# A four-layer cross-attention network with expert layers: expert outputs of layers 1 and 3 written to token rows in DRAM by accumulating scatters, weights carried beside the rows, layer 3 dispatched by ranks

## The chip, the core and the metric

The kernel runs on one core of a Trainium2 chip. The metric is device time in microseconds for one execution. Before the change it was 4479.0 as the median of three runs (4478.08 to 4484.96). Names of engines are those of the profile: PE multiplies matrices (PEld loads its weights), DVE, ACT and POOL work on vectors, SP issues DMAs. POOL issues every indirect DMA, that is, a DMA whose rows are addressed by a list of indices.

## What is computed

Four layers work on x, 2048 tokens of 256 float32. Each layer adds a cross-attention over a context of 1601 rows (16, 16, 8 and 16 heads) and then a feed-forward part with experts. A layer norm stands ahead of each. The feed-forward parts of layers 1, 2 and 3 are, cut to what matters here:

```python
# layer 1: top 2 of 8 experts, all pairs kept
topk_values, topk_indices = jax.lax.top_k(x @ router_w, 2)
topk_weights = softmax(topk_values)
h1 = gelu(einsum('bth,efh->btef', x, w1) + b1)
expert_outputs = einsum('btef,ehf->bteh', h1, w2) + b2
out = sum over the two of expert_outputs[chosen] * topk_weights
# layer 2: 8 experts
y = einsum('bsi,eoi->bseo', x, We) + be
out = einsum('bseo,bse->bso', y, gate_sparse)          # two nonzero gates a token
# layer 3: a shared MLP, and top 2 of 16 experts with room for 320 pairs each
pos = (cumsum(oh_e, axis=0) * oh_e).sum(axis=1) - 1    # place of a pair at its expert
within = pos < 320
expert_outputs = vmap(mlp)(expert_inputs, w_gate, w_up, w_down)   # silu(x wg) * (x wu) wd, F = 352
out = x + mlp(x, shared) + sum over the two of expert_outputs[chosen] * vals * within
```

Layer 0 has a shared MLP and 16 experts, all of them computed for all tokens.

## The kernel before

x stays in SBUF as four blocks of 512 tokens (NB = 4), each of four tiles of 128 tokens (NT = 4). PE's order within attention is written out by hand (`tc.manual_schedule`), and so is the interleaving of the next attention's start (`lead`) with the end of a feed-forward part. The rest is ordered by a scheduler at build time. [...]

Layer norm: `norm_rows` (L399) makes the normed rows xn of a block on POOL: rs, pow, then four subtract-and-multiply (L406), one for each tile. PE transposes them (L416), and the router's logits follow (L621). For the last block of a layer nothing else is left for PE to do meanwhile.

Layer 1. `ffn1` sorts the 4096 pairs of token and expert by expert into 40 tiles of 128 places (TL1 = 40, some places empty). PE counts pairs by matmuls of the one-hot matrix (L913 to L916); `locate` (DVE) finds which row of counts a place falls into; `tokens` gathers four rows `rk` of ranks (L1028, POOL) and makes token numbers out of them; `pairs_T` gathers 128 normed rows `xg` (L1047, POOL), PE transposes them (L1055) and DVE copies (L1057). `hidden` is L1067 and the GELU L1075, `down` is L1089; DVE copies the result (L1093), and SP stores it in `ys_dram` (L1094). The expert's weights w1 and w2, 1 MB each, are fetched by indirect DMAs (L966, POOL) two tiles ahead into two buffers each; where the buffer already holds the same expert the indices are out of bounds and nothing moves. In sixteen of the 40 tiles `bias` (L1113) also adds one token tile's combination of expert biases: a transpose (L767), a copy (L769), a matmul (L771) and a sum into x (L772). When all tiles are done, `combine` (L1140) gathers, for each token tile, its two rows of `ys_dram` (L1144, POOL) and adds them with their weights (L1150, DVE). The next attention's `lead` is interleaved with it.

Layer 2. `ffn2` begins with the biases of all sixteen token tiles (`add_biases`, L774, by the same lines L767 to L772) and then computes all experts (L1174).

Layer 3. `ffn3` counts pairs on PE (L1221), finds each pair's place on DVE and scatters token numbers into a `table` in DRAM by 32 indirect DMAs (L1264), each of which waits for the one before, since they write to the same tensor. The shared MLP runs meanwhile (L1305 and L1323). The table is read back as `slots` (L1280). For each of 16 experts, three indirect DMAs gather normed rows (L1338), PE transposes (L1348), `mlp_hidden` runs (L1305, ACT L1309, DVE L1312), then down (L1357), DVE's copy (L1364) and SP's store (L1365). At the end 32 indirect DMAs gather the two results of each token (L1372), DVE adds them (L1378) and SP stores x as the output.

Of the kernel before, what the change touches and what calls it, by code (L numbers as in the profile page):

```python
# [66 lines left out]
def block_stack(ctx: ExitStack, tc: tile.TileContext, I: dict, out: bass.AP):  # L67
# [44 lines left out]
    iota_p = slot_id[:, 0:1]  # L112
    iota_t = const.tile([P, TL1], F32, name="iota_t")
# [285 lines left out]
    def norm_rows(b, mv):  # L399

        rs = small.tile([P, NT], F32, tag="rs", name="rs")
        nc.gpsimd.tensor_scalar(rs, mv[:, :, 1], LN_EPS, None, ALU.add)  # L402
        nc.gpsimd.tensor_tensor(rs, rs, neg_half, ALU.pow)
        xn = act.tile([P, NT, D], F32, tag="xn", bufs=1, name="xn")
        for t in range(NT):
            nc.gpsimd.tensor_scalar(  # L406
                xn[:, t, :], x[b][:, t, :], mv[:, t, 0:1], rs[:, t : t + 1], ALU.subtract, ALU.mult
            )
        return xn
# [21 lines left out]
    def attention(L, W, kT, V, after):  # L431
# [68 lines left out]
        def rows(b):  # L500
            xn[b] = norm_rows(b, mvs.pop(b))
# [158 lines left out]
    def two_hot(eng, cw, i8f, w, E):  # L660

        o = onehots(i8f, 2, E)
        for k in range(2):
            eng.tensor_tensor(o[:, k], o[:, k], w[:, :, k : k + 1].to_broadcast([P, NT, E]), ALU.mult)
# [13 lines left out]
    def weights_tile(b, E):  # L678
        return small.tile([P, NT, E], F32, tag=f"cw{b}", bufs=1, name=f"cw{b}")
# [85 lines left out]
    def add_bias(b, t, cw, be, E):  # L765
        pt = ps_misc()
        nc.tensor.transpose(pt[0:E, 0:P], cw, ident)  # L767
        cT = tmp([P], "cT")
        nc.vector.tensor_copy(cT[0:E, :], pt[0:E, 0:P])  # L769
        po = ps_misc()  # L770
        nc.tensor.matmul(po[:, 0:D], cT[0:E, :], be, start=True, stop=True)  # L771
        nc.vector.tensor_tensor(x[b][:, t, :], po[:, 0:D], x[b][:, t, :], ALU.add)  # L772

    def add_biases(b, cw, be, E):  # L774

        for t in range(NT):
            add_bias(b, t, cw[:, t, :], be, E)
# [19 lines left out]
    def work(name):  # L797
        return act.tile([P, 2, BT], F32, tag="work", bufs=6, name=name)

# [86 lines left out]
    def ffn1(chosen, xn_dram, fill, lead):  # L886
# [6 lines left out]
        b2 = wp.tile([E, D], F32, tag="be", name="b2")  # L893
        nc.sync.dma_start(b2, I["b2"])
# [11 lines left out]
        oh, w = chosen  # L906

        both = act.tile([P, NTT, E], F32, tag="mp", name="both")
        nc.vector.tensor_tensor(both, oh[0], oh[1], ALU.add)
        bothf = both.rearrange("p t e -> p (t e)")  # L910
        NE = NTT * E
        prow, ptot, pin = ps_one(), ps_one(), ps_one()
# [3 lines left out]
        nc.tensor.matmul(pin[:, 0:NE], upper, bothf, start=True, stop=True)  # L916
# [74 lines left out]
        tile_of, row = cut(TL), cut(TL)  # L991
        row_u, tok_u = cut(TL, U32), cut(TL, U32)

        def locate(t0, n):
# [20 lines left out]
            nc.vector.tensor_tensor(rank[:, at], rank[:, at], before, ALU.subtract)  # L1015
            nc.vector.tensor_scalar(tile_of[:, at], tile_of[:, at], NTT - 1.0, None, ALU.min)
# [6 lines left out]
        def tokens(t0, n):  # L1023
# [18 lines left out]
            nc.vector.tensor_scalar(tok[:, 0:n], tok[:, 0:n], T - 1.0, None, ALU.min)  # L1042
            nc.vector.tensor_copy(tok_u[:, at], tok[:, 0:n])

        def pairs_T(t):
            xg = act.tile([P, D], F32, tag="xnT", bufs=5, name="xg")
# [11 lines left out]
            return xT  # L1058
# [24 lines left out]
        ys_dram = dram.tile([TL * P, D], F32, name="ys1_dram")  # L1083

        def down(t, h):
# [7 lines left out]
            nc.vector.tensor_copy(ys, pd[:, 0:D])  # L1093
            nc.sync.dma_start(ys_dram[t * P : (t + 1) * P, :], ys)  # L1094


        place = act.tile([P, NTT, E], F32, tag="mp", name="place")
        nc.vector.tensor_tensor(
            place, pin[:, 0:NE].rearrange("p (t e) -> p t e", e=E), cum, ALU.add
        )  # L1100
        nc.vector.tensor_tensor(place, place, tot, ALU.subtract)
        nc.vector.tensor_tensor(place, place, bc(st, NTT), ALU.add)
        slots = []
        for k in range(2):
            pk = act.tile([P, NTT, E], F32, tag="mp", name="pk")
            nc.vector.tensor_tensor(pk, place, oh[k], ALU.mult)
            sk = cut(NTT)
            nc.vector.tensor_reduce(sk.unsqueeze(2), pk, AX.X, ALU.add)
            sk_u = cut(NTT, U32)
            nc.vector.tensor_copy(sk_u, sk)  # L1110
            slots.append(sk_u)

        def bias(b, t):  # L1113
            at = slice(b * NT + t, b * NT + t + 1)
            cw = tmp([E], "cw_t")
            nc.vector.tensor_scalar(cw, oh[0][:, b * NT + t, :], w[0][:, at], None, ALU.mult)
            nc.vector.scalar_tensor_tensor(cw, oh[1][:, b * NT + t, :], w[1][:, at], cw, ALU.mult, ALU.add)
            add_bias(b, t, cw, b2, E)
# [4 lines left out]
        for t in range(TL + 1):  # L1123
# [5 lines left out]
            if t < TL:  # L1129
                hs[t] = hidden(t, xTs.pop(t))  # L1130
                if t + 2 < TL:
                    fetch(w1s[t % 2], "w1", t + 2)
            if t > 0:
                down(t - 1, hs.pop(t - 1))
                if t + 1 < TL:
                    fetch(w2s[(t - 1) % 2], "w2", t + 1)
            if 8 <= t < 8 + NTT:
                bias(*divmod(t - 8, NT))

        def combine(b, t):  # L1140
            tt = b * NT + t
            y = act.tile([P, 2, D], F32, tag="xnT", bufs=5, name="y")
            for k in range(2):
                nc.gpsimd.indirect_dma_start(  # L1144
                    out=y[:, k, :],
                    out_offset=None,
                    in_=ys_dram,
                    in_offset=bass.IndirectOffsetOnAxis(ap=slots[k][:, tt : tt + 1], axis=0),
                )
                nc.vector.scalar_tensor_tensor(  # L1150
                    x[b][:, t, :], y[:, k, :], w[k][:, tt : tt + 1], x[b][:, t, :], ALU.mult, ALU.add
                )

        with tc.manual_schedule(engines={mybir.EngineType.PE}):
            for tt in range(NTT):
                combine(*divmod(tt, NT))
                if tt >= NT - 1:
                    lead((tt - NT + 1) / (NTT - NT))

    def ffn2(xnT, lead):  # L1160
        E = 8
        be = wp.tile([E, D], F32, tag="be", name="be")
        nc.sync.dma_start(be, I["be"])
# [27 lines left out]
        for b in range(NB):  # L1191
            add_biases(b, cws[b], be, E)
# [9 lines left out]
    SC = [(0, P), (P, 2 * P), (2 * P, CAP)]  # L1202

    def ffn3(xnT, chosen, xn_dram):
        NTT = NB * NT
        TW = E3 * len(SC)

        table = dram.tile([P * TW, 1], I32, name="table")
        zero = const.tile([P, TW], I32, name="zero")
        nc.vector.memset(zero, 0)  # L1210
        nc.sync.dma_start(table.rearrange("(p c) o -> p (c o)", p=P), zero)
        ids = const.tile([P, NTT], I32, name="ids")
        nc.gpsimd.iota(ids, pattern=[[P, NTT]], base=0, channel_multiplier=1)

        oh, idx, w = chosen

        both = act.tile([P, NTT, E3], F32, tag="mp", name="both")
        nc.vector.tensor_tensor(both, oh[0], oh[1], ALU.add)
        bothf = both.rearrange("p t e -> p (t e)")
        pin, ptot = ps_one(), ps_one()  # L1220
        nc.tensor.matmul(pin[:, 0 : NTT * E3], upper, bothf, start=True, stop=True)  # L1221
        nc.tensor.matmul(ptot[:, 0 : NTT * E3], ones, bothf, start=True, stop=True)
# [358 lines left out]
```

## Time and profile before

The profiled execution took 4487.74 us, of which 4486.0 are the span of its instructions; the mean granted clock of PE was 0.959.

| what | us |
|---|---|
| median of three runs | 4479.0 |
| profiled execution, span | 4487.74, 4486.0 |
| busy: PE, DVE, ACT, POOL | 4258.6, 2414.3, 1959.6, 653.1 |
| layer 1, the 40 tiles | 2093.6 to 2416.7 |
| layer 2, biases | 3159.3 to 3188.5 |
| layer 3, table scatters L1264 | 4150.2 to 4231 |
| layer 3, the 16 experts | 4237.9 to 4434 |
| layer 3, gathers, sums and store | 4434 to 4486 |

A row of the profile's timeline gives start, duration, engine, line, operation and operands; in brackets stands how long the engine was idle ahead of it and what released it. A row of windows gives a stretch, its length, each engine's busy time with the number of its instructions in parentheses (PE, PEld, DVE, ACT, POOL), the granted clock of PE, the share of time the DMA engines were busy, and GB/s. The slices give the span in 40 equal parts and the busy share in tenths.

### The profile page before, as it was taken

What the parts mean: (1) busy time and instruction counts of PE and PEld (TensorE: products, weight loads), DVE (VectorE), ACT (ScalarE), POOL (GpSimd) and SP (SyncE); (2) the same over time, 40 slices, a digit from 0 to 9 for tenths busy, and PEclk for the clock granted to TensorE, in tenths of its full rate; (3) what the DMA queues carried; (4) which work ended last, traced back from release to release, by engine and by line L of the source; (5) the groups of instructions that cost most, each with busy time, mean ns of one, the idle gap of its engine ahead of it and who ended that gap; (6) DMA issues with size and microseconds to landing.
All of it is one profiled execution on the core that took longest, in us unless ns stands there. A gap on an engine that the chain in (4) does not pass through costs nothing. (4 is left out here: it accounts for less than half of the span.)

```text
span 4486.0 us, 62975 instructions
## 1 busy us (share of the span) xinstructions
PE 4258.6 (95%) x25100; PEld 1965.4 (44%) x25100; DVE 2414.3 (54%) x4911; ACT 1959.6 (44%) x3690; POOL 653.1 (15%) x833
## 2 busy tenths in 40 slices
PE   8999999999999999998996999999999999998695
PEld 4333333366543333336885433334443333333463
DVE  5776776324677776753222544451486777673122
ACT  1666655511156655662221234343016766665010
POOL 2000100100000010004445100012000001001323
PEclk8999999999999999999998799999899999999897
DMA  2000000000000000002453000000000000000144
GB/s 75 3 3 4 3 3 6 3 23 1 3 3 6 4 8 3 11 6 70 163 167 89 10 5 3 5 6 3 3 16 3 4 3 8 11 1 10 32 148 116
DMA packets 64429, 117.31 MB, mean 26 GB/s; under 512 B 20110, under 2 KB 41478, under 8 KB 59528
## 3 DMA queue, kind: packets, MB, share of 16 engines
q1 hardware_dynamic: 43272, 58.12, 4.3%
q0 software_dynamic: 20864, 55.18, 4.1%
q8 instruction: 198, 3.24, 0.3%
q14 instruction: 95, 0.78, 0.1%
HBM read 138.37 MB, written 16.88 MB: 35 GB/s over the span
## 5 line engine op out<-in xcount | busy, mean ns | idle before, releaser
L284 DVE TENSOR_REDUCE mx<-ps_m 128x1 f32<-128x512 f32 x2688 | 1699.9, 685 | 672.2 <-PE ps_m L277 437.5
L325 PE MATMUL ps_s<-q,kT 32*128 32x512 f32 (+2 forms) x5824 | 1721.0, 623 | 0.7 <-DVE mx L284 0.6
L277 PE MATMUL ps_m<-kT,q 32*128 32x512 f32 x5376 | 1604.8, 644 | 29.9 <-DMA q<-qc 18.5
L335 ACT ACTIVATE e<-ps_s 128x512 f32<-128x512 f32 (+1 forms) x2080 | 1110.7, 599 | 890.5 <-PE ps_s L325 694.4
L343 PE MATMUL ps_acc<-e,V 128*32 128x512 f32 (+2 forms) x5824 | 928.5, 609 | 6.2 <-ACT a L524 5.7
L325 PEld LDWEIGHTS ps_s<-q,kT 32*128 32x128 f32 (+2 forms) x5824 | 576.4, 180 | 671.7 <-DVE mx L284 397.0
L277 PEld LDWEIGHTS ps_m<-kT,q 32*128 32x128 f32 x5376 | 580.4, 188 | 504.4 <-issue 383.1
L333 ACT ACTIVATE e<-ps_s,mcol 128x512 f32<-128x512 f32 (+1 forms) x832 | 514.8, 686 | 224.3 <-PE ps_s L325 143.8
L343 PEld LDWEIGHTS ps_acc<-e,V 128*32 128x32 f32 (+2 forms) x5824 | 160.6, 112 | 640.6 <-issue 508.4
L266 POOL MEMSET mp<- 128x512 f32 x64 | 33.2, 525 | 1846.7 <-PE ps_m L315 1836.2
L1075 ACT ACTIVATE h<-ps_h,w 128x128 f32<-128x128 f32 x320 | 91.1, 372 | 217.7 <-issue 138.2
L854 DVE SCALAR_TENSOR_TENSOR x<-ps_m,cw,x 128x256 f32<-128x256 f32 x256 | 111.1, 479 | 102.1 <-PE ps_m L846 99.1
L402 POOL TENSOR_SCALAR rs<-mv 128x4 f32<-128x4 f32 x32 | 7.6, 239 | 1050.5 <-DVE mv L394 1050.5
L406 POOL TENSOR_SCALAR xn<-x,mv,rs 128x256 f32<-128x256 f32 x128 | 156.0, 1231 | 3.5
L1067 PE MATMUL ps_h<-xT,w 128*128 128x128 f32 x1280 | 153.2, 279 | 0.4 <-issue 0.4
L817 ACT ACTIVATE h<-ps_h 128x512 f32<-128x512 f32 x80 | 47.7, 597 | 242.3 <-PE ps_h L816 242.3
L1067 PEld LDWEIGHTS ps_h<-xT,w 128*128 128x128 f32 x1280 | 149.6, 195 | 0.8 <-issue 0.5
L301 DVE TENSOR_REDUCE mx<-ps_m 128x4 f32<-128x260 f32 x224 | 80.4, 423 | 126.0 <-PE ps_m L293 126.0
L1089 PE MATMUL ps_m<-w,h 128*128 128x256 f32 x640 | 144.6, 379 | 0.0
L1089 PEld LDWEIGHTS ps_m<-w,h 128*128 128x128 f32 x640 | 118.6, 190 | 14.5
L1312 DVE TENSOR_TENSOR h<-ps_h,sg 128x320 f32<-128x320 f32 (+3 forms) x60 | 31.8, 530 | 168.1 <-PE ps_h L1305 121.6
L816 PE MATMUL ps_h<-xnT,up 128*128 128x512 f32 x256 | 117.9, 604 | 0.0
(286 smaller groups left out, 3179.6 us busy)
## 6 DMA issues: line engine op xcount, KB each, us to landing
q<-qc SPq DMA_DIRECT2D x192, 32.0 KB
gu<-in_w_gate SPq DMA_DIRECT2D x16, 352.0 KB
gu<-in_w_up SPq DMA_DIRECT2D x16, 352.0 KB
ys_dram<-ys SPq DMA_DIRECT2D x40, 128.0 KB
xn_dram<-xn SPq DMA_DIRECT2D x8, 512.0 KB
dn<-in_w_down SPq DMA_DIRECT2D x16, 256.0 KB
ys<-ys_sb SPq DMA_DIRECT2D x32, 128.0 KB
x<-in_x SPq DMA_DIRECT2D x4, 512.0 KB
```

The costliest lines, as they stand in the source:

```text
L277: nc.tensor.matmul(pm, q1[at : at + 32, t * P : (t + 1) * P], kT[at : at + 32, g, KB[kb] : KB[kb + 1]], start=True, stop=True,)
L284: nc.vector.tensor_reduce(mx[:, t, j, kb : kb + 1], pm, AX.X, ALU.max)
L325: nc.tensor.matmul(sp, kT[j * S : (j + 1) * S, g, c * P : c * P + cw], q2[j * S : (j + 1) * S, :], start=True, stop=True,)
L333: nc.scalar.activation(e[0:cw], sp, AF.Exp, bias=mcol[0:cw, c : c + 1])
L335: nc.scalar.activation(e[0:cw], sp, AF.Exp)
L343: nc.tensor.matmul(acc[j * S : (j + 1) * S, :], V[0:cw, c, h * (d + 1) : h * (d + 1) + S], es[j // 2][0:cw, j % 2, :], start=(c == 0), sto ...
L406: nc.gpsimd.tensor_scalar(xn[:, t, :], x[b][:, t, :], mv[:, t, 0:1], rs[:, t : t + 1], ALU.subtract, ALU.mult)
L816: nc.tensor.matmul(pu, u(c), xnT[b][:, c, :], start=(c == 0), stop=(c == 1))
L854: nc.vector.scalar_tensor_tensor(x[b][:, t, :], pd[:, i * D : (i + 1) * D], cws[b][:, t, e0 + e + i : e0 + e + i + 1], x[b][:, t, :], ALU. ...
L1067: nc.tensor.matmul(pu[:, (f - f0) * P : (f - f0 + 1) * P], w1[:, c * F1 + f * P : c * F1 + (f + 1) * P], xT[:, c, :], start=(c == 0), stop ...
L1075: nc.scalar.activation(h[:, f, :], pu[:, (f - f0) * P : (f - f0 + 1) * P], AF.Gelu, bias=w1[:, 2 * F1 + f : 2 * F1 + f + 1],)
L1089: nc.tensor.matmul(pd[:, 0:D], h[:, f, :], w2[:, f * D : (f + 1) * D], start=(f == 0), stop=(f == 7))
```

## The change

Rows in DRAM get wider: behind the 256 normed values of a token stand its weights for all experts (8 in layer 1, 16 in layer 3), so that whoever gathers a row has the weight too. 128 zero rows behind the tokens are spare: empty places point there. A second tensor, `acc_dram`, holds x; experts' results, already multiplied with the weight, are added to it by indirect DMAs with `compute_op=ALU.add`, 40 in layer 1 and 48 in layer 3, each waiting for the one before. After layer 1, x is read back from it; after layer 3 it is copied to the output, DRAM to DRAM. The gathers and sums at the end of both layers, `ys_dram` and the place of each pair are gone.

Layer 3 finds its tokens as layer 1 does, by gathering ranks (40 gathers), and gathers rows for two experts at a time, five tiles of 128 for 2 x 320 places. The tile in the middle belongs half to one and half to the other. Its counting now stands behind the first block of the shared MLP.

The biases of layers 1 and 2 are added in routing, one block at a time: one transpose, an ACT copy, four matmuls and four sums. `norm_rows` takes the engine for the rows: DVE for the last block after each attention, and for the first block at the start of each.

```diff
-    def norm_rows(b, mv):
+    def norm_rows(b, mv, eng):
...
-            nc.gpsimd.tensor_scalar(
+            eng.tensor_scalar(
...
+    def add_biases(b, cw, be):
         pt = ps_misc()
+        nc.tensor.transpose(pt[:, 0:P], cw.rearrange("p t e -> p (t e)"), ident)
+        cT = small.tile([P, P], F32, tag="cT", bufs=1, name="cT")
+        nc.scalar.copy(cT, pt[:, 0:P])
+        pos = [ps_misc() for t in range(NT)]
         for t in range(NT):
-            add_bias(b, t, cw[:, t, :], be, E)
+            at = slice(t * 32, t * 32 + 8)
+            nc.tensor.matmul(pos[t][:, 0:D], cT[at, :], be[at, :], start=True, stop=True)
+        for t in range(NT):
+            nc.vector.tensor_tensor(x[b][:, t, :], pos[t][:, 0:D], x[b][:, t, :], ALU.add)
...
+    def spare(tok, gone, tok_u):
...
+        nc.vector.tensor_scalar(tok, tok, T - 1.0, None, ALU.min)
+        nc.vector.tensor_scalar(other, tok, -1.0, spare_row, ALU.mult, ALU.add)
+        nc.vector.tensor_tensor(other, other, gone, ALU.mult)
+        nc.vector.tensor_tensor(tok, tok, other, ALU.add)
+        nc.vector.tensor_copy(tok_u, tok)
...
         def pairs_T(t):
-            xg = act.tile([P, D], F32, tag="xnT", bufs=5, name="xg")
+            xg = act.tile([P, D + E], F32, tag="xnT", bufs=5, name="xg")
...
-            return xT
+            w8 = tmp([E], "w8")
+            nc.vector.tensor_tensor(w8, xg[:, D : D + E], oht[:, t, :], ALU.mult)
+            weight = small.tile([P, 1], F32, tag="weight", bufs=4, name="weight")
+            nc.vector.tensor_reduce(weight, w8, AX.X, ALU.add)
+            return xT, weight
...
-            nc.vector.tensor_copy(ys, pd[:, 0:D])
-            nc.sync.dma_start(ys_dram[t * P : (t + 1) * P, :], ys)
+            nc.vector.tensor_scalar(ys, pd[:, 0:D], weight, None, ALU.mult)
+            nc.gpsimd.indirect_dma_start(
+                out=acc_dram,
+                out_offset=bass.IndirectOffsetOnAxis(ap=tok_u[:, t : t + 1], axis=0),
+                in_=ys,
+                in_offset=None,
+                compute_op=ALU.add,
+            )
...
-            if 8 <= t < 8 + NTT:
-                bias(*divmod(t - 8, NT))
...
+        for b in range(NB):
+            nc.sync.dma_start(
+                x[b], acc_dram[b * BT : (b + 1) * BT, :].rearrange("(t p) d -> p t d", p=P)
+            )
         with tc.manual_schedule(engines={mybir.EngineType.PE}):
-            for tt in range(NTT):
-                combine(*divmod(tt, NT))
-                if tt >= NT - 1:
-                    lead((tt - NT + 1) / (NTT - NT))
+            lead(1.0)
...
-        for b in range(NB):
-            add_biases(b, cws[b], be, E)
```

Layer 3, the new functions in short, and the order in which they run:

```python
def tokens(k):
    at = slice(5 * k, 5 * k + 5)
    rk = act.tile([P, 5, P], F32, tag="o_tok", bufs=2, name="rk")
    for c in range(5):
        nc.gpsimd.indirect_dma_start(out=rk[:, c, :], in_=ranks_dram, ...)
    nc.vector.tensor_tensor(rk, rk, rank[:, at].unsqueeze(2).to_broadcast([P, 5, P]), ALU.is_le)
    ...
def pairs(k):
    ...
    for c in range(5):
        nc.gpsimd.indirect_dma_start(out=xg[c], in_=xn_dram, ...)
    ws = small.tile([P, 6], F32, tag="ws", name="ws")
    for to, c, src, two in (...):
        nc.vector.tensor_copy(ws[0 : src.stop - src.start, to : to + 1], xg[c][src, e : e + 1])
    return xg, ws
def down(k, two, hs, dn, ws):
    ...
    for i, (n, tok) in enumerate(parts):
        pd = ps_one()
        ys = act.tile([P, D], F32, tag="mp", name="ys")
        ...
        nc.vector.tensor_scalar(ys[0:n, :], pd[0:n, 0:D], w, None, ALU.mult)
        nc.gpsimd.indirect_dma_start(out=acc_dram, ..., in_=ys[0:n, :], compute_op=ALU.add)
...
for b in range(NB):
    if b == 1:
        cum = counts()
        locate(cum)
        tokens(0)
        tokens(1)
    hs = mlp_hidden(gu, [xnT[b][:, c, :] for c in range(2)], BT)
    ...
    nc.sync.dma_start(acc_dram[b * BT : (b + 1) * BT, :].rearrange("(t p) d -> p t d", p=P), x[b])
xg, ws = pairs(0)
for k in range(E // 2):
    xT = pairs_T(xg)
    ws_now = ws
    if k + 2 < E // 2:
        tokens(k + 2)
    if k + 1 < E // 2:
        xg, ws = pairs(k + 1)
    for two in range(2):
        gu, dn = load_mlp("w", 2 * k + two)
        hs = mlp_hidden(gu, [xT[c][:, two * CAP : (two + 1) * CAP] for c in range(2)], CAP)
        down(k, two, hs, dn, ws_now)
for b in range(NB):
    nc.sync.dma_start(out[b * BT : (b + 1) * BT, :], acc_dram[b * BT : (b + 1) * BT, :])
```

## The prediction

> **What bounds the kernel now.** I read the slices first, then busy time by stage, then single stretches.
>
> ```profile
> span 4486.0 us, 62975 instructions
> PE 4258.6 (95%) x25100; PEld 1965.4 (44%) x25100; DVE 2414.3 (54%) x4911; ACT 1959.6 (44%) x3690; POOL 653.1 (15%) x833
> PE   8999999999999999998996999999999999998695
> POOL 2000100100000010004445100012000001001323
> ...
> 2416.70:2438.70 22.00, 0.06 (x2) 0.04 (x1) 7.58 (x21) 0.00 (x0) 13.20 (x16) 0.57 0.34 102
> 2438.70:2497.80 59.10, 43.75 (x107) 25.18 (x108) 36.54 (x71) 1.86 (x3) 35.87 (x33) 0.53 0.18 54
> 3158.00:3189.00 31.00, 24.18 (x56) 9.88 (x55) 9.85 (x32) 0.52 (x2) 0.00 (x0) 0.60 0.00 1
> 4186.00:4237.00 51.00, 19.72 (x67) 11.94 (x65) 4.84 (x7) 1.79 (x3) 18.41 (x19) 0.72 0.09 25
> 4237.00:4434.00 197.00, 194.21 (x768) 126.23 (x768) 43.56 (x96) 34.46 (x80) 43.13 (x46) 0.98 0.45 130
> 4434.00:4486.00 52.00, 0.00 (x0) 0.00 (x0) 15.74 (x33) 0.00 (x0) 30.91 (x32) 0.53 0.41 123
> ```
>
> PE is 95% busy, so only what PE does or waits for counts. The dips are at the combine of layer 1 (2417 to 2498), the biases of layer 2 (3158 to 3189, at a granted clock of 0.60) and layer 3: waiting for the slot table until 4237, and a tail of 52 us after PE's last matmul. In layers 1 and 3 POOL, which issues every indirect DMA, is busiest.
>
> ```profile
> 4194.99 0.97 POOL L1264 DMA_INDIRECT table<-ids,at_u  x1 [1.46 <-DMA table<-ids,at_u]
> 4197.39 0.97 POOL L1264 DMA_INDIRECT table<-ids,at_u  x1 [1.44 <-DMA table<-ids,at_u]
> ...
> 4237.91 0.69 PE L1348 MATMUL ps_m<-ident,xg 128*128 128x128 f32 x2 [32.18 <-DMA xg<-xn_dram,slots]
> 4241.28 9.06 PE L1305 MATMUL ps_h<-xT,gu 128*128 128x320 f32 x24 [0.41 <-issue]
> ...
> 4255.51 6.76 PE L1305 MATMUL ps_h<-xT,gu 128*128 128x320 f32 x24
> 4438.56 0.95 POOL L1372 DMA_INDIRECT y<-ys,row_u  x1 [0.30 <-issue]
> ```
>
> Two prices: indirect DMAs that wait for each other start 2.4 us apart; those that don't, 1.27 (0.95 + 0.30). After a long idle stretch the first hidden layer takes 9.06 instead of 6.76, so a stall costs about 2 us besides its own length.
>
> **Layer norm rows on DVE.**
>
> ```profile
> 2047.11 0.69 PE L416 MATMUL ps_m<-ident,xn 128*128 128x128 f32 x2 [4.75 <-POOL xn L406]
> 2048.32 0.69 PE L416 MATMUL ps_m<-ident,xn 128*128 128x128 f32 x2 [0.52 <-POOL xn L406]
> ```
>
> For a layer's last block PE waits 4.75 + 3 x 0.52 for POOL's four rows of 1.21. A 128x256 copy on DVE takes 0.42, so four rows come 3.1 sooner; rs and pow stay on POOL. DVE has nothing else there. I take -3 per layer, four times: **-12** (0 to -14). The first block's rows matter only after layer 1, and are in that tail.
>
> **Biases.** In layer 1 sixteen tiles of the expert loop take 8.79 instead of 7.25 (transpose 0.27, wait 0.59, matmul 0.69): 24.6 leave. In layer 2, 3159.3 to 3188.5 holds nothing but sixteen transposes and biases: 29.2 leave. Added: per block one transpose 0.27, an ACT copy (about 0.4), four matmuls of 0.43: 2.5 each for three blocks inside attention, 7.5. The last block has no cover. In layer 1 its weights are made while DVE finishes routing anyway (PE already idles 2.76 before L913): 4.5. In layer 2 PE used to start the next layer's K/V projections at once, and now stands queued behind the bias; logits to cw took 3124.5 to 3130.6 with a projection's copies of some 1.6 between, so 4.5 + 2.7 = 7.2. Layer 1: -24.6 + 12 = **-12.6**; layer 2: -29.2 + 14.7 = **-14.5** (each within 6).
>
> **Layer 1 loop.** Without biases it is 323.1 - 24.6 = 298.5. POOL's four tiles held 16 indirect DMAs (4 ranks, 4 rows, 8 weight fetches) and now hold 20, with four accumulating scatters: 20 x 1.27 = 25.4 of 29.0. That fits as a sum, but the queue is in order: a scatter waits for the evacuation of its tile, and behind it stand the next fetch of w1, three rank gathers and the rows; DVE's weight products wait for those gathers and stand ahead of the evacuations. Following one period through both queues with the rows' durations gives 30.1 to 30.5 instead of 29.0: +12 over ten. At seven expert changes w1 is issued late, where 1 MB needs about 3.4 (the first four took 13.5): I take 1 each, 7 in all, less 1 for what was already late before: **+18**. Bounds: 0 (all covered) and +53 (rival d).
>
> **End of layer 1.** The 40 stores of ys, 32 gathers and 32 DVE sums go. After PE's last matmul come evacuation, scatter, a reload of x, statistics and rows. Evacuation to landing about 6, reload about 4 (a quarter of those 13.5), statistics, pow and rows on DVE about 5: the query projection at +15.6 instead of +26.7 (2416.7 to 2443.4), -11. In the stretch after, PE idles 59.1 - 43.75 = 15.4, much of it because the maxima share DVE with L1150; I take 12 of it. **-23** (-10 to -28).
>
> **Layer 3, dispatch.** Gone: 32 chained table scatters and the read of slots. Added: five count matmuls after the shared MLP's first block (about 4147), 16 sums (3.1 by L1226) and a locate, then 40 rank gathers that don't wait for each other: 4159 + 40 x 1.27 + 2 = 4212. Every one of them stands ahead of the first rows in POOL's queue: five gathers and 2.7 to land, first hidden layer at 4222 instead of 4241.3: **-19** (-8 to -24). The shared MLP is over at about 4197, so some 25 of idle PE stay.
>
> **Layer 3, loop.** Sixteen experts of 11.93 = 191. Rows are gathered five per pair of experts instead of six, the store of ys becomes 48 accumulating scatters, each waiting for the one before. Let L be their spacing. No row of this trace has an accumulate. Lower bound: 2.4, the table's scatters, with 4 bytes a row. Nearest for 1 KB rows: a gather is used by DVE 2.7 after its start (4437.29 to 4440.02); a scatter adds a read of the target. Upper bound: two such trips and the issue, 2 x 2.7 + 0.95 = 6.4. With weights filling DMA to 0.45 I take L = 4.0, nearer the single trip. POOL per pair: 6 scatters, of which one overlaps the row gathers, 5L + 6.4 = 26.4 against PE's 23.87: +2.5, over 8 pairs +20. Or, seen from DVE: the copy of the pair's last weight waits for row gather c4, which is queued behind a scatter, and h stands behind it: a scatter's trip less the 1.1 that PE is ahead, 2.9 in six pairs, 17. These are one delay, not two; with lost clock in six places, 1.5 each: **+28** (+8 at L = 2.4; +116 at L = 6.4, where POOL needs 38.4, 14.5 over PE's).
>
> [...]
>
> **Layer 3, tail.** Gone: last store, 32 gathers of y (40 us), 32 sums, the store of out. Added: the last scatters, about 10 after PE's last matmul at L = 4, then four copies of 512 KB from DRAM to DRAM; 130 GB/s at a share of 0.45 makes some 290, 2 MB in 7 plus 2 to land. 20 instead of 52: **-32** (-25 to -36).
>
> **Sum**: -12 - 12.6 - 14.5 + 18 - 23 - 19 + 28 - 32 = -67. The profiled span 4486.0 becomes 4419; its execution took 4487.74, 8.7 above the median 4479.0 of the three runs, so I expect **4412** as median.
>
> **Rivals.**
> (b) The scatter chain decides. At L = 6, POOL needs 36.4 per pair, 12.5 over PE's 23.87: +100 instead of +28, tail +6: -67 + 78 = +11, 4490; at 6.4 4507. From L = 5.7 on the change loses. For it: every table scatter waited, some 3.8 apart instead of 2.4 under load; the target is read too. Against: POOL's wait in the typical row is only 1.46. 0.18.
> (c) All is covered: L at most 2.5, the layer 1 queue as fast as PE. +8 and 0 instead of +28 and +18: -105, 4374. For it: POOL is 15% busy over the span, table scatters 2.4. Against: in layer 1 it is 45%, and order, not sum, decides. 0.14.
> (d) Layer 1's fetches come late: seven changes at 6 + 1.6 (clock; L1067 took 5.37 instead of 3.74 after a 1.64 stall) make +53 instead of +7: -21, 4458. For it: each scatter sits between two fetches in one queue. Against: two buffers. 0.13.
> My forecast gets 0.50, with its own range 4385 to 4440; 0.05 is left for a mixture near no change. Slices from (c) to (b) give 4360 to 4488. I take 0.2% (9 us) as what a measurement can tell. Faster: forecast, (c) and most of (d): 0.75; slower: 0.18; same: 0.07.
>
> **What would show it.** PE's wait before the first xg transpose of layer 3 near 20; spacing of L1416's scatters near 4, and pairs near 27; nothing but four copies after a tail of 20; the layer 1 loop near 317, with POOL fetches just before use; layer 2's biases as one 7 us stop after the logits. Wrong if a scatter takes 6 or more, or if rank gathers are still running at 4230.

## The result, and the profile after

The changed kernel takes 4519.5 us (median of four runs, 4517.94 to 4520.16) where the kernel before takes 4481.98 beside it (four runs, 4478.08 to 4487.5): a ratio of 1.0082, 95% interval 1.0065 to 1.01. It is 0.8% slower. The prediction was 4412, and faster. In the profiled executions the span went from 4486.0 to 4518.5, +32.5 where the sum said -67.

The page of the changed kernel, first lines of busy time and slices:

```profile
span 4518.5 us, 62932 instructions
PE 4261.5 (94%) x25064; PEld 1986.0 (44%) x25064; DVE 2432.1 (54%) x5024; ACT 1959.9 (43%) x3700; POOL 705.8 (16%) x890
PE   7999999999999999998788899999999999999786
PEclk8999999999999999998898799999899999999988
```

PE has 36 instructions fewer than before and is busy for as long as before (4258.6). The dip of layer 1's end (the "6" in the twenty-second slice before) has gone, but there is a new one, "87888", over the expert loop of layer 1, and the last slices ("786") are little fuller than before ("695"). The same stretches in windows: start and end, length, busy time of PE, PEld, DVE, ACT and POOL, granted clock, DMA share, GB/s.

```profile
2115.10:2495.60 380.50, 310.59 (x2000) 288.96 (x2000) 84.69 (x314) 91.98 (x321) 208.53 (x193) 0.90 0.45 118
2495.60:2509.50 13.90, 0.00 (x0) 0.00 (x0) 3.06 (x12) 0.00 (x0) 3.92 (x5) 0.61 0.71 213
...
3169.20:3175.60 6.40, 1.69 (x10) 0.78 (x10) 3.50 (x28) 0.50 (x2) 0.29 (x1) 0.50 0.03 6
4203.00:4254.00 51.00, 28.81 (x85) 17.16 (x83) 26.61 (x83) 2.37 (x5) 33.33 (x35) 0.80 0.55 88
4254.00:4495.80 241.80, 203.34 (x743) 131.99 (x742) 50.51 (x136) 31.64 (x79) 102.12 (x79) 0.89 0.46 107
4495.80:4518.50 22.70, 0.02 (x1) 0.00 (x0) 0.97 (x2) 0.00 (x0) 4.56 (x3) 0.57 0.38 107
```

In both expert loops (first and fifth row) PE is idle for 70 and 38 us at a granted clock of 0.9; before, the loop of layer 3 had 0.98 and 2.8 us of idle PE. The gap after layer 1 is 13.9 instead of 22, the tail 22.7 instead of 52. The stages are cut at PE's instructions (the start of the first or the end of the last of a group), and the prediction's terms are put into them:

| stage | before | after | change | predicted |
|---|---|---|---|---|
| start to first K/V matmul | 18.0 | 26.2 | +8.3 | 0 |
| layer 0, attention, routing and shared MLP | 978.9 | 974.3 | -4.6 | -3 (rows) |
| layer 0 experts, layer 1 attention and routing | 1061.4 | 1077.4 | +16.0 | +9 (biases +12, rows -3) |
| counts to first rows | 35.3 | 37.2 | +1.9 | 0 |
| layer 1 loop | 323.1 | 380.4 | **+57.3** | -6.6 (biases -24.6, loop +18) |
| end of layer 1, layer 2 attention to last logits | 707.8 | 673.7 | -34.1 | -18.5 (end -23, biases +7.5, rows -3) |
| logits to layer 2 experts | 64.0 | 43.8 | -20.2 | -22 (biases -29.2 + 7.2) |
| layer 2 experts to layer 3's last logits | 945.9 | 945.6 | -0.3 | -3 (rows) |
| logits to first expert of layer 3 | 106.9 | 95.5 | -11.4 | -19 |
| layer 3 experts | 192.5 | 241.7 | **+49.2** | +28 |
| tail | 52.2 | 22.7 | -29.5 | -32 |

The rows add up to +32.5. Two thirds of the miss of 100 is one row, the layer 1 loop; the loop of layer 3 is 21 of it. Of the other rows, three are 7.0 to 8.3 worse than their terms (the start, layer 1's attention and routing, layer 3's dispatch), the end of layer 1 is 16 better, and the rest is within 3.

**Layer 1 loop.** The groups of PE in it: busy time, mean ns of one, then idle time ahead of them and what ended it.

```profile
L1087 PE MATMUL ps_h<-xT,w 128*128 128x128 f32 x1280 | 165.9, 293 | 0.8 <-issue 0.8
L1107 PE MATMUL ps_m<-w,h 128*128 128x256 f32 x640 | 144.7, 379 | 0.0
L1070 PE MATMUL ps_m<-ident,xg 128*128 128x128 f32 x80 | 18.0, 312 | 70.3 <-DMA xg<-xn_dram,pad 70.3
```

The last of these in the kernel before:

```profile
L1055 PE MATMUL ps_m<-ident,xg 128*128 128x128 f32 x80 | 16.3, 285 | 0.7 <-DMA xg<-xn_dram,pad 0.7
```

The waiting is for gathered rows, none of it for the experts' weights: 70.3 us, of which 67.6 lie in eight stops of 6.9 to 11.1, one for every four tiles, and the rest in two of 1.3 and 1.4 at the start. The timeline of POOL at one of them, with DVE's last step in finding the token numbers of the next rows, and then PE's:

```profile
2280.27 0.17 DVE L819 CAST pad<-tok 128x4 uint32<-128x4 f32 x1
2290.30 1.62 POOL L1112 DMA_INDIRECT acc_dram<-ys,pad  x1 [1.82 <-DVE ys L1111]
2292.23 1.05 POOL L981 DMA_INDIRECT w<-in_w,pad  x1 [0.30 <-issue]
2293.58 0.97 POOL L1062 DMA_INDIRECT xg<-xn_dram,pad  x1 [0.31 <-issue]
```

```profile
2285.88 3.62 PE L1107 MATMUL ps_m<-w,h 128*128 128x256 f32 x16
2299.73 0.69 PE L1070 MATMUL ps_m<-ident,xg 128*128 128x128 f32 x2 [10.23 <-DMA xg<-xn_dram,pad]
```

PE has finished the last tile of a set of four. The rows of the next four can only be gathered now, because their gathers (L1062) stand in POOL's queue behind the scatter (L1112) of that last tile, which waits for DVE's evacuation, and behind a weight fetch. Their token numbers had been ready for 13 us (11.3 to 13.5 in the eight stops), so it is the order of the queue that holds them back, and not their input. Until the first has landed, PE has nothing to do.

### The profile page after: what moved, and what is told of

Same layout as the page of the kernel before. It is cut to its first block, busy times and chain, and to the rows that moved or that the text cites. A ratio compares the mean times of both kernels' runs of the same rounds, so it can differ in the third digit from the quotient of the medians.

```text
span 4518.5 us, 62932 instructions
## 1 busy us (share of the span) xinstructions
PE 4261.5 (94%) x25064; PEld 1986.0 (44%) x25064; DVE 2432.1 (54%) x5024; ACT 1959.9 (43%) x3700; POOL 705.8 (16%) x890
## 5 line engine op out<-in xcount | busy, mean ns | idle before, releaser
L1087 PE MATMUL ps_h<-xT,w 128*128 128x128 f32 x1280 | 165.9, 293 | 0.8 <-issue 0.8
L1087 PEld LDWEIGHTS ps_h<-xT,w 128*128 128x128 f32 x1280 | 163.3, 210 | 1.2 <-issue 1.2
L1319 ACT ACTIVATE sg<-ps_h 128x320 f32<-128x320 f32 (+3 forms) x60 | 28.1, 468 | 231.7 <-PE ps_h L1315 231.7
L1111 DVE TENSOR_SCALAR ys<-ps_m,weight 128x256 f32<-128x256 f32 x40 | 19.3, 484 | 192.3 <-PE ps_m L1107 188.1
L1406 PE MATMUL ps_m<-dn,h 128*128 128x256 f32 (+3 forms) x288 | 89.7, 463 | 34.9 <-DVE h L1322 34.9
```

Source lines behind the costliest of these rows:

```text
L1087: nc.tensor.matmul(pu[:, (f - f0) * P : (f - f0 + 1) * P], w1[:, c * F1 + f * P : c * F1 + (f + 1) * P], xT[:, c, :], start=(c == 0), stop ...
L1406: nc.tensor.matmul(pd[0:n, 0:D], hs[f][:, at : at + n], dn[0 : fhi - flo, f, :], start=(f == 0), stop=(f == len(FC) - 1),)
```

## Experiments

All are edits of the changed kernel. Spans are those of the profiled execution, against 4518.5. Experiments 1 to 9 ran once each. All runs of the kernel before lie between 4477.3 and 4494.8, and layer 0, which experiments 1 to 8 hardly touch, took 969.8 to 983.7 in them; so the stage that an edit is about says more than the span. A pair of layer 3 is the mean distance from the first transpose of one pair of experts to that of the next.

**1. Bookkeeping not ahead of the start.** Before, PE's first matmul was at 17.99. After, POOL begins with 64 small instructions that belong to layer 3 and wait for nothing; the copies of `wk` (L190) that PE waits for stand behind them. POOL's groups in the first 30 us, and PE's first matmul:

```profile
L1239 POOL TENSOR_SCALAR book<-slot_id 128x2 f32<-128x2 f32 (+1 forms) x32 | 8.1, 255 | 2.1
L1242 POOL MEMSET book<- 128x2 f32 (+1 forms) x32 | 3.3, 104 | 1.0
```

```profile
26.25 1.71 PE L218 MATMUL ps_m<-ctxT,wk 128*128 128x401 f32 x2 [26.25 <-POOL wk L190]
```

```diff
-            nc.vector.tensor_copy(rank, slot_id[:, 0:NC])
+            late = small.tile([P, NC], F32, tag="late", bufs=1, name="late")
+            nc.gpsimd.tensor_scalar(late, bothf[:, 0:NC], 0.0, None, ALU.mult)
+            nc.gpsimd.tensor_tensor(late, late, slot_id[:, 0:NC], ALU.add)
...
-                        rank[ps_, cols], slot_id[ps_, cols], float(-CAP * (2 * k + two)), None, ALU.add
+                        rank[ps_, cols], late[ps_, cols], float(-CAP * (2 * k + two)), None, ALU.add
```

> The 64 small POOL operations that prepare layer 3's slot numbers are tied to layer 3's routing, so they can't run at the start. Theory (in the changed kernel they stand in POOL's queue at 10.9 to about 21 us, ahead of the first layer norm's pow and of the copies of wk): PE's first matmul comes at 18 to 20 us instead of 26.25 and everything after is about 7 earlier, span near 4511. Rival (the four loads of zero rows on SP, which delay wk by some 5, are what counts): the first matmul stays at 23 to 26 and the span gains 0 to 3.

The first matmul came at 19.70, 6.5 sooner, and the 64 ran at 3818 to 3834, beside attention. The span was 4520.9 all the same, where 4511 was expected. Layer 0 took 979.3 instead of 974.3, which is within its spread, and layer 3 needed 101.4 from its last logits to its first expert instead of 95.5, since POOL and DVE were put into another order there: PE's stops in the shared MLP are 27.5 instead of 22.2. The local cause is shown for 6.5 of the 8.3; taken alone the gain does not reach the end.

**2. Layer 1, rows gathered two tiles ahead.** The order of POOL and DVE written by hand; the four rank gathers of a set stay together.

```diff
-            if t + 1 < TL:
-                xTs[t + 1] = pairs_T(t + 1)
+        with tc.manual_schedule(engines={mybir.EngineType.Pool, mybir.EngineType.DVE}):
...
+                if t + 2 < TL:
+                    xgs[t + 2] = rows_of(t + 2)
+                if t + 1 < TL:
+                    xTs[t + 1] = pairs_T(t + 1, xgs.pop(t + 1))
```

> Layer 1's expert loop in the changed kernel with POOL and DVE in a written order: the gather of normed rows is issued two tiles ahead, one per tile, between the fetch of w2 and the next fetch of w1. All instructions stay. Theory (four gathers of rows stand behind a scatter that waits for the last evacuation, so PE waits some 7 to 11 us every fourth tile): PE's waits for xg fall from 70.3 us in ten to under 10, the loop from about 379 us to 300 to 310, the span by 65 to 80 to about 4445. Rival (POOL's throughput or slow accumulating scatters bind; 20 indirect DMAs, scatters at 1.6 us): PE's waits only move to another operand, the loop stays over 345 and the span over 4480.

A miss: PE still waited 54.3 us for xg, and the loop took 368.6; the span was 4501.4. Most gathers were issued only 3 us ahead of their use, which just sufficed (in the changed kernel's loop they land after 2.8, median). Nine stood behind a burst of four rank gathers (4 x 1.27), and PE waited for these nine 43.2 of the 54.3 us.

**3. Layer 1, rows three tiles ahead, rank gathers one to a tile.**

```diff
+                if t + 3 < TL:
+                    xgs[t + 3] = rows_of(t + 3)
...
+                    fetch(w1s[t % 2], "w1", t + 2)
+                if rks is not None:
+                    rank_row(rks, t % 4, t - t % 4 + 8 + t % 4)
+                if t > 0:
+                    down(t - 1, *hs.pop(t - 1))
```

> Layer 1 alone: the gather of a tile's rows is issued three tiles before its use, the four rank gathers of a set are spread one to a tile two sets ahead, and the order of GpSimd and VectorE is written by hand. Theory A (the gather comes too late because it stands on GpSimd behind a scatter that waits for the experts, and behind bursts of rank gathers): TensorE's waits for xg fall from 70.3 us to under 10, the half-clock windows behind these stalls go, the loop falls from about 380 us to 295-310 and the span by 60-80 to 4440-4460. Rival B (GpSimd is full: per tile a gather, a weight load, a scatter and a rank gather take about as long as the tile's 7.25 us): the loop stays above 340 with other waits in place of xg's. Layer 3 is the changed kernel's and keeps pairs of 31 us.

Span 4430.8. The PE groups of this loop:

```profile
L1105 PE MATMUL ps_h<-xT,w 128*128 128x128 f32 x1280 | 150.6, 276 | 0.0
L1125 PE MATMUL ps_m<-w,h 128*128 128x256 f32 x640 | 144.7, 379 | 0.0
L1088 PE MATMUL ps_m<-ident,xg 128*128 128x128 f32 x80 | 15.6, 277 | 2.5 <-DMA xg<-xn_dram,pad 2.5
```

and one tile of POOL's queue, which repeats every 7.25 us on average:

```profile
2283.06 0.96 POOL L1077 DMA_INDIRECT xg<-xn_dram,pad  x1 [0.31 <-PE ps_h L1105]
2284.33 1.00 POOL L981 DMA_INDIRECT w<-in_w,pad  x1 [0.30 <-issue]
2285.64 0.96 POOL L1040 DMA_INDIRECT rk<-ranks_dram,pad  x1 [0.30 <-issue]
2287.03 1.81 POOL L1130 DMA_INDIRECT acc_dram<-ys,pad  x1 [0.44 <-DVE ys L1129]
2289.15 1.02 POOL L981 DMA_INDIRECT w<-in_w,pad  x1 [0.31 <-issue]
2290.48 0.97 POOL L1077 DMA_INDIRECT xg<-xn_dram,pad  x1 [0.31 <-PE ps_m L1125]
```

The same instructions, five to a tile, fit into the same queue with almost no stop of PE: 292.8 us for the loop, below the lower end that was expected. The difference to the changed kernel's 380.4, 87.6, is accounted for but for 2 us by two rows: 67.8 less waiting for xg, and 17.7 less in matmuls (150.6 + 15.6 against 165.9 + 18.0), which ran at half clock (granted 0.50) behind each stop. Rival B, that POOL is too full for this loop, falls, though narrowly: the five with their gaps of 0.3 take 7.1 of the 7.25.

**4. Scatters that overwrite.** The adding is left out of both layers.

```diff
                 in_offset=None,
-                compute_op=ALU.add,
```

> The scatters of layers 1 and 3 overwrite in place of adding (the output lacks the sums of the experts: the adding is left out). Theory A (adding makes the issue and the landing longer): the issue on GpSimd falls from 1.6 us to about 0.95, the spacing of chained scatters from 4.5 us to 3.0-3.5, pairs of layer 3 from 31 to 27-29 us, the layer 1 loop from 380 to 350-365, span 4450-4490. Theory B (issue and landing belong to an indirect write as such): 1.4-1.6 us and 4.3-4.6 us as before, pairs 30.5-31.5, span within 10 us of the changed kernel's 4518.

POOL's scatters in the layer 1 loop, of the changed kernel and then of this one:

```profile
L1112 POOL DMA_INDIRECT acc_dram<-ys,pad x40 | 64.7, 1617 | 57.3 <-DVE ys L1111 51.6 <-issue 2.9 <-DVE xT L1072 2.8
```

```profile
L1112 POOL DMA_INDIRECT acc_dram<-ys,pad x40 | 41.0, 1025 | 58.7 <-DVE ys L1111 55.8 <-issue 2.9
```

Chained scatters of layer 3, of the changed kernel and then of this one:

```profile
4360.15 1.59 POOL L1416 DMA_INDIRECT acc_dram<-ys,tok_u  x1 [4.57 <-DVE ys L1415]
4364.77 1.57 POOL L1416 DMA_INDIRECT acc_dram<-ys,tok_u  x1 [3.02 <-DVE ys L1415]
4369.37 1.43 POOL L1416 DMA_INDIRECT acc_dram<-ys,tok_u  x1 [3.03 <-DVE h L1322]
```

```profile
4368.56 0.98 POOL L1415 DMA_INDIRECT acc_dram<-ys,tok_u  x1 [2.22 <-DMA acc_dram<-ys,tok_u]
4371.77 0.90 POOL L1415 DMA_INDIRECT acc_dram<-ys,tok_u  x1 [2.22 <-DMA acc_dram<-ys,tok_u]
```

Adding costs 0.6 us of POOL's time for each scatter (1617 against 1025 ns) and makes the trip from issue to landing 3.8 to 3.9 instead of 2.5; a chain runs at 4.60 instead of 3.21. So the price itself is as Theory A had it, and so is the span of 4483.2. But the loops hardly follow: 372.3 against 380.4 in layer 1, where PE still waits 60.8 for xg, which misses the expected 350 to 365; and pairs of 29.4 against 31.3 in layer 3, just above the expected range. The two loops and the tail make 26.7 of the 35.3 by which the span fell; the rest lies in stages that the edit does not touch. Dearer scatters are the smaller part; where they stand is the larger.

**5. Layer 3, order alone.** The copies of the weights `ws` are made at the start of the pair that uses them, and POOL issues the five gathers of a pair ahead of the six scatters.

```diff
             for k in range(E // 2):
+                ws_now = weights_of(k, xg)
                 xT = pairs_T(xg)
-            ws_now = ws
...
                 if k + 1 < E // 2:
-                xg, ws = pairs(k + 1)
+                    xg = pairs(k + 1)
```

> Layer 3's loop in the changed kernel with POOL and DVE in a written order: the weight copies ws of a pair stand at the pair's start, when its rows have long landed, instead of ahead of the h products of the pair before; POOL does five row gathers, then six scatters. Scatters still wait for each other. Theory A (the chain of scatters binds: 4 x 4.5 + 2 x 3.9 and gathers that don't fit into its waits): a pair takes 28 to 30 us instead of 31.0, span about 4500 to 4512. Theory B (DVE's order binds: h behind ws behind a gather): 24 to 25 a pair, span about 4465.

**6. Layer 3, chain alone.** The scatters of one expert do not wait for each other: its tokens all differ, and empty places of its three tiles go to different spare rows.

```diff
+                this = f"sc{2 * k + two}"
+                if i > 0:
+                    tc.declare_no_dep(sc, group=this, reason="rows of one expert differ")
+                for old in last_scatters:
+                    tc.add_manual_dep(sc, old.name, ...)
```

> Layer 3's loop in the changed kernel, where the three scatters of one expert no longer wait for each other (their tokens differ, and empty places get spare rows of their own); the first of an expert waits for all of the expert before. DVE's program is as before. Theory A (the chain binds): a pair takes 24 to 26 us instead of 31.0, span about 4470. Theory B (DVE's order binds): PE still waits 3 to 4 for h at each pair's first expert, 27 to 28.5 a pair, span about 4490 to 4500.

**7. Layer 3, both.** With a third buffer for ys, the order of the shared MLP and the dispatch by hand, half of the rank gathers moved into the loop, and a small memset between the scatters of one expert.

```diff
+        def hook_of(b):
+            def hook(f):
+                at = (b, f)
+                if at == (2, 1):
+                    tokens_of(0, rks.pop(0))
+                    xgs[0] = pairs(0)
+                    rks[2] = rank_rows(2)
...
+        with tc.manual_schedule(engines={mybir.EngineType.Pool, mybir.EngineType.DVE}):
...
+                    if two == 0 and k + 4 < E // 2:
+                        rks[k + 4] = rank_rows(k + 4)
```

> Layer 3 alone: scatters of one expert do not wait for each other, weights are multiplied in at the pair's start, a third buffer for the products, and the order of the shared MLP and the dispatch is written by hand (four sets of rows found before the loop, the other four inside it, the first gather of rows right behind the first set). Theory A (both the chain of scatters and VectorE's and GpSimd's order cost; neither alone was enough): pairs of 24-25 us in place of 31.3, no waits of the shared MLP for h (22.2 us before), the first expert's matmul 25-30 us earlier than 4254, span 4430-4450. Rival B (GpSimd's issues alone set the pair: 11 indirect transfers of 1.2-1.6 us and their waits): pairs stay at 27-29 us and the span is 4465-4490.

The two groups of PE in the loop of layer 3, hidden layer and output layer: the changed kernel, then 5, 6 and 7 (of 6 the output layer alone).

```profile
L1315 PE MATMUL ps_h<-xT,gu 128*128 128x320 f32 (+1 forms) x384 | 108.4, 438 | 3.6 <-DVE ys L1415 3.4
L1406 PE MATMUL ps_m<-dn,h 128*128 128x256 f32 (+3 forms) x288 | 89.7, 463 | 34.9 <-DVE h L1322 34.9
```

```profile
L1315 PE MATMUL ps_h<-xT,gu 128*128 128x320 f32 (+1 forms) x384 | 123.5, 477 | 25.0 <-DVE ys L1417 22.7 <-DVE ws L1391 1.9 <-ACT xT L1377 0.2
L1408 PE MATMUL ps_m<-dn,h 128*128 128x256 f32 (+3 forms) x288 | 68.4, 386 | 8.6 <-DVE h L1322 8.6
```

```profile
L1416 PE MATMUL ps_m<-dn,h 128*128 128x256 f32 (+3 forms) x288 | 85.1, 449 | 28.2 <-DVE ws L1385 19.8 <-DVE h L1330 8.3
```

```profile
L1327 PE MATMUL ps_h<-xT,gu 128*128 128x320 f32 (+1 forms) x384 | 108.2, 437 | 0.6 <-DVE ys L1407 0.5
L1398 PE MATMUL ps_m<-dn,h 128*128 128x256 f32 (+3 forms) x288 | 68.4, 386 | 0.0
```

In the changed kernel PE waits for h, the product that DVE makes, 34.9 us. DVE's timeline at one of the stops shows why:

```profile
4352.95 0.31 DVE L1377 COPY ws<-xg 64x1 f32<-64x1 f32 x2 [1.15 <-DMA xg<-xn_dram,tok_u]
4355.77 0.15 DVE L1377 COPY ws<-xg 128x1 f32<-128x1 f32 x1 [2.52 <-DMA xg<-xn_dram,tok_u]
4355.85 0.49 DVE L1322 TENSOR_TENSOR h<-ps_h,sg 128x320 f32<-128x320 f32 x1
```

and POOL's, of the scatter and of the gather in question:

```profile
4345.67 1.56 POOL L1416 DMA_INDIRECT acc_dram<-ys,tok_u  x1 [2.43 <-DVE ys L1415]
4351.41 0.94 POOL L1359 DMA_INDIRECT xg<-xn_dram,tok_u  x1 [0.30 <-PE ps_h L1315]
```

The copy at 4355.77 waits for a gather that was queued on POOL, the fourth in a row, behind a scatter that itself had waited; h stands behind the copy, and PE idles 4.65 us. With the order mended (5), these waits fall to 8.6, and 22.7 come back as waits for ys: ys has two buffers, which a scatter holds until it has landed (in the changed kernel DVE waits 13 times, 35.4 us in all, for a scatter's landing before it writes ys), so I read this as the chain. With the chain cut (6), 28.2 stay, most for the copies. Either edit alone takes a pair from 31.3 to 28.7 (5, as Theory A had it; span 4505.4) and 29.1 (6, more than either theory allowed; span 4494.1). Both together, with the lesser edits of 7, take it to 22.8, less than the 23.87 of the kernel before, with scatters of one expert 1.7 to 1.95 apart, and the loop from 241.7 to 182.4: 37.9 less waiting, and 21.3 less in L1398 (386 ns for a matmul instead of 463). The stops of the shared MLP (22.2 us in the changed kernel) fall to 4.7, and the first expert starts 74.8 behind the last logits instead of 95.5. Span 4422.7, below the expected 4430 to 4450; 86.6 of the 95.8 that it fell are in layer 3 and the tail. Which of the lesser edits of 7 weighs what was not tried; the third buffer for ys above all could take part of what stands here as the chain.

**8. Without the biases.**

```diff
             if n in (1, 2):
                 yield
-                add_biases(b, cw, be)
```

> Left out: the expert biases of layers 1 and 2 in the routing (transpose of the weights, copy, four matmuls and four sums for each block), so the output lacks them. Theory A (the prediction's price, 12 us in layer 1 and 14.7 in layer 2, each block 2.5 inside attention and the last block 4.5 to 7.2): the layer 1 counts come 10-14 us earlier than 2077.9, the layer 2 projections start 6-7 us sooner after the logits, span 4488-4496. Rival B (each stop for a weight also starts a stretch at half clock, three in layer 1): 20 us or more in layer 1 alone, span 4470-4485. Rival C (the biases are cheap and layer 1 is late for other reasons): under 6 us in layer 1.

Span 4479.6. From the last logits to the experts of layer 2: 34.9 instead of 43.8, so the last block costs 8.9 there. For the other three blocks the stage ahead of these logits shows nothing (673.8 against 673.7), but it can't show a few us: with the same instructions it takes 669.6 to 675.0 in the other kernels at a granted clock of 0.94 and 680.2 at 0.93, and without the biases the clock was 0.93. Layer 0's experts to the counts of layer 1: 1058.1 instead of 1077.4, so 19.3, between A and B. Twelve of that are clock. In the changed kernel, 46.9 us of this stage are granted 0.50 (three stretches of 6.83 us inside attention, at 1727.3, 1898.0 and 1935.5, among them; the first and the last begin just behind a bias's stop of 0.62); without biases, 22.6. But five of the other kernels, with the same instructions in this stage (3 to 7), need 1065.4 to 1065.7, have 23.1 to 23.5 at 0.50, and no such stretch inside attention. Against these the biases cost 7.4; experiments 1, 2 and 10 have the stretches, and need 1074.6 to 1077.5. Why the clock drops behind the stops of some kernels and not of others stays open.

**9. Rows on POOL again.**

```diff
-            xn[b] = norm_rows(b, mvs.pop(b), nc.vector if b == 0 else nc.gpsimd)
+            xn[b] = norm_rows(b, mvs.pop(b), nc.gpsimd)
```

> Undone: the rows of the layer norm of the first and last block go to GpSimd again. Theory A (the prediction's price): the last block's four waits come back, about 3 us for each layer, two of the four visible before layer 1's counts; layer 1's counts 5-8 us later than 2077.9, span 4526-4534. Rival B (the rows were worth 2 us or less a layer): span within 6 us of 4518.5, and TensorE's waits for xn in a last block 4.7 + 3 x 0.5 in place of about 4.

Span 4535.5, +17.0, and the counts at 2086.3, +8.4. Of this, 4.3 are the start (the first block's rows now stand ahead of the copies of `wk` on POOL, and PE's first matmul is at 30.57); the next three stages move by +13, -9 and, in layer 2's attention, +13, along with the time at half clock, so I go by the waits. PE's waits for xn over the whole kernel, us and times, of the changed kernel and of this one:

```profile
  DVE xn L408: 30.0, 5
```

```profile
  POOL xn L408: 43.0, 20
```

The rows are worth 13.0 by PE's waits, close to the 12 of the prediction: 9.9 at the last blocks of the four layers, which the 12 were for, and 3.1 behind layer 1.

**10. Together:** the edits of 1, 3 and 7, and the zeros for the spare rows loaded later.

```diff
-    zero = work("zero").rearrange("p c n -> p (c n)")
...
     with tc.manual_schedule(engines={mybir.EngineType.PE}):
         parts["lead"](1.0)
+    zero = work("zero").rearrange("p c n -> p (c n)")
...
```

> The layer 1 order, the layer 3 order and the late bookkeeping at the start together, and the zero rows loaded later. If the costs are where the theories put them, they add up: layer 1 -60 to -75, layer 3 -70 to -85, start -5 to -8: span 4350-4385, faster than both kernels (ratio to the kernel before 0.97-0.98). Rival: what one stage gains is given back in the next (later clock drops, late weight loads): above 4420.

4333.46 us (median of four, 4327.63 to 4339.64) against 4485.64 of the kernel before: a ratio of 0.9663, interval 0.9644 to 0.9682. That is faster than the expected 4350 to 4385. The gains add up by stages: against the changed kernel the loop of layer 1 takes 84.6 less (87.6 in 3), layer 3 from its last logits on 84.8 less (86.6 in 7), and the start 11.3 less, 180.7 of the 185.9 by which the span fell. That the spans of 3 and 7 fell by 183.5 together is in part luck: both hold 12 of clock ahead of layer 1's counts, which this kernel does not have, and it has the 11.3 of the start, which they do not. Of its page and of its windows (layer 1 loop, layer 3 loop, tail):

```profile
span 4332.6 us, 62960 instructions
PE   8999999999999999999999899999899999999998
```

```profile
2103.00:2398.90 295.90, 293.60 (x2000) 274.40 (x2000) 84.06 (x320) 91.85 (x321) 211.62 (x193) 0.99 0.55 151
...
4133.70:4316.20 182.50, 181.67 (x742) 123.01 (x742) 64.27 (x189) 31.60 (x79) 125.21 (x132) 1.00 0.67 149
4316.20:4332.60 16.40, 0.00 (x0) 0.00 (x0) 0.48 (x1) 0.00 (x0) 2.90 (x3) 0.60 0.50 148
```

In both loops PE is idle for less than 3 us. The idea of the change was sound; the order in which its parts were queued took more than it gave. What the kernel before would gain by the same care for order was not tried.

## Why the prediction was wrong

**Where it failed: the layer 1 loop.** "That fits as a sum, but the queue is in order" was right, and naming the scatter that waits for the evacuation, with gathers behind it, was the right picture. The step that failed is the next: "Following one period through both queues with the rows' durations gives 30.1 to 30.5 instead of 29.0". A period of four tiles took 38.0 (380.4 / 10). I followed the scatter's delay into the fetch of w1, and priced that (1 us for each of seven changes, or 6 in rival d). PE never waited for a weight. What came late was the next set's rows, whose four gathers the queue holds behind the last tile's scatter; PE then waits for the evacuation, the scatter, a fetch, a gather and its landing in a row, 8.5 us on average, eight times, and loses 17.7 more to the clock behind these stops. The issue of the scatter, taken as 1.27 like any other indirect DMA, was 1.62 + 0.3, but experiment 4 shows that this is the smaller part. Rival d came nearer in size, for the wrong transfer. Its +53, the upper bound, was too low: without its biases the loop grew by 380.4 - 298.5 = 82.

**Layer 3 loop: a size, and one false step.** L was taken as 4.0 and measured 4.60 for 128 rows (3.9 for 64). Put into the prediction's own 5L + 6.4, this gives 29.4 for a pair and +44 for the loop; measured were 31.3 and +49.2. Both delays that the forecast named, the chain and DVE's order, were there. "These are one delay, not two" was wrong: experiments 5 and 6 each remove one and find the other behind it, nearly as long. The +28 itself does not follow from its parts: they give 17 + 9 or 20 + 9. The upper bound of 6.4, in which the target's read is a second trip of 2.7, was an estimate that no run shows: adding made the trip 3.8 to 3.9 instead of 2.5 (experiment 4). In 6 and 7 the scatters of one expert touch different rows and start 1.7 to 3.3 and 1.7 to 1.95 apart.

**Not foreseen: the start.** +8.3, of which experiment 1 gives 6.5 to POOL instructions of layer 3 that have no input to wait for. The prediction counted what the new parts of layer 3 do in layer 3, and did not ask when they are issued.

**Layer 3 dispatch**: -11.4 instead of -19. The counts stood 17.8 behind the last logits on PE instead of 12.6. From there the first rank gather took 12.6, where 12 were priced, and the 40 started 1.26 apart, as priced (4188.99 to 4238.08). The wait ahead of the first xg, "near 20", did not come as such: PE spent 22.2 in stops of the shared MLP, whose h stood on DVE behind operations that waited for rank gathers. That "the shared MLP is over at about 4197" was thus the false step.

**Right, or nearly:** the rows (12; 11.6 by PE's waits of 49.6 and 30.0, less the 8.0 at the end of layer 1, and 9.4 of it at the four last blocks that were meant), the tail (-29.5 for -32), and layer 2's last block (one stop of 6.4 us; 8.9 instead of 7.2 by experiment 8). The end of layer 1 is -34.1 in its stage, 15.6 more than predicted. The surplus is luck: PE's idle time in the stage fell by 20.2 (57.9 to 37.7), less than the 26 that were predicted with the rows, and its busy time, predicted to rise by 7.5, fell by 13.9 (649.9 to 636.0) with 25 matmuls more, at a granted clock of 0.94 instead of 0.90. In layer 1 the routing's biases cost 19.3 in this kernel instead of 12, of which 7.4 show without the stretches at half clock.

## What to carry to other kernels

In the layer 1 loop an indirect DMA that waits for a result, put into the one queue that also issues the next inputs, delayed those by the whole way from the last matmul to the landing, and PE stood for 8.5 us on average, eight times; check for each queue what stands behind a waiting entry and when its consumer needs it, and issue inputs as many tiles ahead as buffers allow. If one of two stops is removed and the time moves little, look for a second of the same length behind it before giving up the theory. Work without inputs was put first by the scheduler here, ahead of what the first matmul needs (6.5 us by experiment 1); look at the start of each queue for it.

## What the runs showed of the hardware that was not expected

In the layer 1 loop an accumulating scatter of 128 rows of 1 KB held POOL for 1.62 us instead of the 1.03 of experiment 4, and landed after 3.9 us (3.8 in layer 3) instead of 2.5. In the changed kernel's routing and loop of layer 1 the stretches at half clock (granted 0.50) last 3.41, 6.83, 10.24, 13.65 or 17.07 us, all multiples of 3.41. In the loop such a stretch began in each of the eight stops, 3.0 to 4.5 us after PE had stopped, and ended 3.0 to 5.6 us after PE had started again; with one at the start they make 78.5 us at half clock, which cost 17.7 us of matmul time besides the 70.3 of waiting.
